# A graph attention and mixture-of-experts layer: an earlier first product, sums of exponentials made in all rows of a head's output, and a rearranged end of routing

## The chip, the cores and the metric

The kernel runs on one core of one Trainium2 chip. A core has five engines with queues of their own: TensorE (PE) multiplies matrices, VectorE (DVE) and ScalarE (ACT) compute on tiles, GpSimd (POOL) here mostly gathers and scatters rows by index, SyncE (SP) issues transfers. Tiles in SBUF have 128 partitions (rows); products land in PSUM. The metric is the device time of one execution in microseconds. A profiled execution of the kernel before took 2289.92 us, an unprofiled one 2153.45 us: all views of the trace belong to the longer, profiled one, and nothing in them tells where the difference lies.

## The reference

The first half is attention over a graph, with 8 heads of 64, on 4096 nodes of 512 features; the second is a feed-forward layer with 8 experts, of which each node uses two.

```python
def _L0_gnn_ref(node_matrix, adjacency_matrix, Wks, Wqs, Wvs, Wo):
    adj = jnp.maximum(adjacency_matrix, eye)
    q = jnp.einsum('nd,hdk->hnk', node_matrix, Wqs)      # k and v likewise
    scores = jnp.einsum('hqk,hmk->hqm', q, k) * kd ** (-0.5)
    scores = scores + IDENTITY_BIAS * eye - MASK_VAL * (1.0 - adj)
    att = jax.nn.softmax(scores, axis=-1)
    return jnp.einsum('hqm,hmk,hko->qo', att, v, Wo)

def _L0_ffn_ref(x, Wg, bg, W1, b1, W2, b2):
    logits = xf @ Wg + bg
    topk_scores, topk_idx = jax.lax.top_k(logits, 2)
    topk_w = jax.nn.softmax(topk_scores, axis=-1)
    h = jax.nn.gelu(jnp.einsum('nd,edh->neh', xf, W1) + b1, approximate=False)
    y = jnp.einsum('neh,ehf->nef', h, W2) + b2
    # the two chosen experts' rows of y, weighted by topk_w and added

x = x + _L0_gnn_ref(_layernorm(x), adj, ...)
x = x + _L0_ffn_ref(_layernorm(x)[None], ...)[0]
```

The graph is sparse. The kernel finds, for each tile of 128 query nodes, which nodes are neighbours of any of them, and gathers only those.

## The kernel before

The kernel has four stages. Stage one normalizes x, turns it, projects keys and values (to `kv_d` in memory) and queries (to `qT_d`), and beside this loads the adjacency matrix (32 pieces of 2 MB) and makes lists of neighbours from it, and packed masks. Stage two is the attention: 363 items, one for each query tile with itself (c < 0) and 331 with 128 listed key nodes each; an item is "full" if its keys concern all 128 queries of the tile, or "half" if only 64 of them. The end of a query tile (sums, reciprocal, output product, routing) is spread in pieces over the six items after its last; those of routing are jobs. The turn ends routing: rows are scattered to their expert's place in `xs_d`, blank rows are put after each expert's last, and a table tells each tile of 128 rows its expert and first row. The experts work off 69 such tiles.

`pk` and `kT` are an item's turned keys in PSUM and SBUF; `ps_e` is a pool of two PSUM tiles that the ends of tiles and the jobs share. Cuts are marked with `# ...`.

```python
# stage one: loads and the first block
xts = {}
def load_x1(i):
    xts[i] = work.tile([P, D], F32, tag="xt", bufs=6, name=f"xt_{i}")
    nc.sync.dma_start(out=xts[i], in_=x[ts(i, P), :])
for i in range(TPB):
    load_x1(i)
for n, src, queue in (("k", Wks, nc.scalar), ("v", Wvs, nc.scalar), ("q", Wqs, nc.sync)):
    for c in range(DC):
        queue.dma_start(out=w[n][:, c], in_=src[ts(c, P), :])
nc.sync.dma_start(
    out=wo, in_=Wo.rearrange("h k o -> (h k) o").rearrange("(c p) o -> p c o", p=P)
)
nc.sync.dma_start(out=wg[:, :, :E], in_=Wg.rearrange("(c p) e -> p c e", p=P))
nc.sync.dma_start(out=bg_sb, in_=bg.partition_broadcast(P))
# ...
def project_kv(b, t):
    i = b * TPB + t
    row = work.tile([P, 2, H * KD], F32, tag="kv", name=f"kv_{i}")
    for s, n in enumerate("kv"):
        pv = ps.tile([P, H * KD], F32, tag="mm", name=f"p{n}_{i}")
        for c in range(DC):
            nc.tensor.matmul(
                pv, xTs[b][:, c, ts(t, P)], w[n][:, c, :],
                start=(c == 0), stop=(c == DC - 1),
            )
        nc.scalar.copy(row[:, s], pv)
    nc.sync.dma_start(out=kv_d[ts(i, P), :], in_=row.rearrange("p s d -> p (s d)"))
# ...
for t in range(TPB):
    tokens_1(t)
    if t == 0:
        tokens_2(t)
        tokens_3(t)
for t in range(1, TPB):
    tokens_2(t)
    tokens_3(t)
for t in range(TPB):
    load_x1(TPB + t)
list_constants()
nc.sync.dma_start(out=out[N : N + P, :], in_=blank[:, :D])
# ...
def pack():
    i, c = ready.pop(0)
    m = work.tile([P, P], F32, tag="mask", bufs=5, name=f"pm_{i}_{c}")
    gather_mask(m, i, c)
    packed[i, c] = len(packed)
    nc.sync.dma_start(out=packed_at(i, c), in_=mask_part(m, i, c))
# ...
# keys of the masks, in lists_of
u = slice(at[i] + u0, at[i] + u1)
k = key[:, u0 - t0 : u1 - t0]
if h is None:
    nc.gpsimd.tensor_scalar_add(mask_of[:, u], k, float(i * (N + 1)))
else:
    nc.gpsimd.tensor_scalar(
        mask_of[:, u], k, 2.0, float(2 * i * (N + 1) + h),
        op0=ALU.mult, op1=ALU.add,
    )
# ...
# stage two: an item's keys are turned, its scores, exponentials and masks, its values
half_q = single.tile([P, 2, Q4], F32, name="half_q")
nc.vector.memset(half_q, 0.0)
spread = single.tile([P, NP, P], F32, name="spread")
nc.vector.memset(spread, 0.0)
for j in range(2):
    nc.vector.memset(half_q[:, j, j * Q4 // 2 : (j + 1) * Q4 // 2], 1.0)
for p in range(NP):
    u, j = divmod(p, 2)
    for r in range(2):
        row = (2 * u + r) * Q4 + j * Q4 // 2
        nc.vector.tensor_copy(
            spread[:, p, r * KD : (r + 1) * KD],
            ident[:, row : row + 1].to_broadcast([P, KD]),
        )
# ...
def turn(n):
    kT[n] = work.tile([P, NP, P], F32, tag="kT", bufs=3, name=f"kT_{n}")
    pk = ps_k.tile([P, 2, TB], F32, tag="k", name=f"pk_{n}")
    for p in range(NP):
        for r in range(2):
            half = slice(r * KD, (r + 1) * KD)
            nc.tensor.transpose(
                pk[:, r, ts(p, KD)], kv[n][half, ts(p, P)], ident[half, half]
            )
    nc.scalar.copy(
        kT[n].rearrange("k p (r j) -> k r p j", r=2),
        pk[:, :, : NP * KD].rearrange("k r (p j) -> k r p j", p=NP),
    )
# ... scores(n): products with q_in, then in ScalarE the exponentials of s into e
def masked(n):
    i, c = items[n]
    e, m = es[n], mask.pop(n)
    # ...
    nc.vector.tensor_mul(e, e, m.unsqueeze(1).to_broadcast(e.shape))
# ...
def values(n):
    i, c = items[n]
    e = es.pop(n)
    if c < 0:
        po[i] = ps_o.tile([P, NP, P], F32, tag="o", name=f"po_{i}")
    v = kv.pop(n)[:, H * KD :]
    q = queries(i, c)
    for h in range(H):
        p, r = divmod(h, 2)
        nc.tensor.matmul(
            po[i][r * KD : (r + 1) * KD, p, q], v[:, ts(h, KD)], e[:, h, :],
            start=(c < 0 and p == 0), stop=(c == listed[i] - 1),
            skip_group_check=True,
        )
    if c >= 0:
        nc.vector.tensor_add(acc[i][:, :, q], acc[i][:, :, q], e)
# ...
# pieces of a query tile's end, k items after its last
def piece(i, k):
    g = group_of[i]
    i0, m = groups[g]
    j = i - i0
    if k == 1:
        sums[i] = ps_e.tile([P, P], F32, tag="e", name=f"sums_{i}")
        a = acc.pop(i)
        for t in range(2):
            for q in range(4):
                u, r = divmod(q, 2)
                nc.tensor.matmul(
                    sums[i][q * Q4 : (q + 1) * Q4], half_q[:, t],
                    a[:, 2 * (2 * u + t) + r, :], start=(t == 0), stop=(t == 1),
                    tile_position=(0, q * Q4), skip_group_check=True,
                )
    if k == 2:
        rinv[i] = single.tile([P, P], F32, tag="rinv", name=f"rinv_{i}")
        nc.vector.reciprocal(rinv[i], sums[i])
        test = single.tile([P, P], F32, tag="test", name=f"test_{i}")
        nc.scalar.activation(test, sums.pop(i), AF.Copy, accum_out=fine[:, i, 0:1])
    if k == 3:
        rb[i] = ps_e.tile([P, NP, P], F32, tag="e", name=f"rb_{i}")
        for p in range(NP):
            nc.tensor.matmul(rb[i][:, p], spread[:, p], rinv[i], start=True, stop=True)
        test = single.tile([P, P], F32, tag="test", name=f"test2_{i}")
        nc.scalar.activation(test, rinv.pop(i), AF.Copy, accum_out=fine[:, i, 1:2])
    if k == 4:
        nc.vector.tensor_mul(osb[i], osb[i], rb.pop(i))
# ...
def later(n):
    busy = False
    for n0, i in left:
        piece(i, n - n0)
        busy = busy or n - n0 in (1, 3, 5)
    if jobs and not busy:
        then = jobs.pop(0)()
        if then:
            first_of_step.append(then)
# ...
if n + 3 < len(items):
    turn(n + 3)
if n + 2 < len(items):
    scores(n + 2)
values(n)
if c == listed[i] - 1:
    osb[i] = single.tile([P, NP, P], F32, tag="o", name=f"o_{i}")
    nc.scalar.copy(osb[i], po.pop(i))
later(n)
if n + 2 < len(items):
    masked(n + 2)
if c == listed[i] - 1:
    left.append((n, i))
# ...
# the end of routing
def finish_routing(pool, psum, blank):
    pn = psum.tile([P, E], F32, name="pn")
    nc.tensor.matmul(pn, ones, count, start=True, stop=True)
    many = pool.tile([P, E], F32, name="many")
    nc.vector.tensor_copy(many, pn)
# ...
past = pool.tile([P, NB, E], F32, name="past_e")
nc.vector.tensor_tensor(
    past, nth.unsqueeze(2).to_broadcast([P, NB, E]),
    upto.unsqueeze(1).to_broadcast([P, NB, E]), op=ALU.is_ge,
)
expert = pool.tile([P, NB], F32, name="expert")
nc.vector.tensor_reduce(expert, past, axis=AX.X, op=ALU.add)
nc.vector.tensor_mul(past, past, tiles_e.unsqueeze(1).to_broadcast([P, NB, E]))
nc.vector.tensor_reduce(first, past, axis=AX.X, op=ALU.add)
nc.vector.tensor_sub(first, nth, first)
nc.vector.tensor_scalar_mul(first, first, float(P))
nc.vector.scalar_tensor_tensor(
    first, expert, float(R), first, op0=ALU.mult, op1=ALU.add
)
nc.vector.tensor_scalar_min(first, first, float(E * R))
nc.vector.tensor_scalar_min(expert, expert, float(E - 1))
nc.vector.tensor_add(many, many, start_e)
nc.vector.tensor_copy(table[:, :NB], expert[:1])
nc.vector.tensor_copy(table[:, NB : 2 * NB], first[:1])
nc.vector.tensor_copy(table[:, 2 * NB :], many[:1])
nc.vector.tensor_add(first, first, number.to_broadcast([P, NB]))
nc.sync.dma_start(out=xs_d[E * R : E * R + P, :], in_=blank)
for e in range(E):
    last = nc.values_load(
        table[:, 2 * NB + e : 2 * NB + e + 1], engines=(SP,), min_val=e * R,
        max_val=e * R + N, skip_runtime_bounds_check_because=why,
    )
    s = nc.sync.dma_start(out=xs_d[bass.ds(last, P), :], in_=blank)
    for t in scatters:
        tc.declare_no_dep(s.ins, t.ins, reason="other rows")
    scatters.append(s)
```

The whole kernel:

Of the kernel before, what the change touches and what calls it, by code (L numbers as in the profile page):

```python
# [10 lines left out]
F32 = mybir.dt.float32  # L11
BF16 = mybir.dt.bfloat16
# [8 lines left out]
P = 128  # L21
# [22 lines left out]
def kernel(  # L44
# [106 lines left out]
    nc.gpsimd.iota(start_e, pattern=[[R, E]], base=0, channel_multiplier=0,  # L151
# [3 lines left out]
    for e in range(1, E):  # L155
# [9 lines left out]
    nth = const.tile([P, NB], F32, name="nth")  # L165
    nc.gpsimd.iota(nth, pattern=[[1, NB]], base=0, channel_multiplier=0,
                   allow_small_or_imprecise_dtypes=True)
# [4 lines left out]
    table = const.tile([1, 2 * NB + E], I32, name="table")  # L172
# [100 lines left out]
    with tc.tile_pool(name="wqkv", bufs=1) as wp, tc.tile_pool(name="p1", bufs=3) as work, tc.tile_pool(  # L273
# [12 lines left out]
        def load_x1(i):  # L286
            xts[i] = work.tile([P, D], F32, tag="xt", bufs=6, name=f"xt_{i}")
            nc.sync.dma_start(out=xts[i], in_=x[ts(i, P), :])

        for i in range(TPB):  # L290
            load_x1(i)
        for n, src, queue in (("k", Wks, nc.scalar), ("v", Wvs, nc.scalar), ("q", Wqs, nc.sync)):
            for c in range(DC):
                queue.dma_start(out=w[n][:, c], in_=src[ts(c, P), :])
        nc.sync.dma_start(
            out=wo, in_=Wo.rearrange("h k o -> (h k) o").rearrange("(c p) o -> p c o", p=P)
        )
        nc.sync.dma_start(out=wg[:, :, :E], in_=Wg.rearrange("(c p) e -> p c e", p=P))
        nc.sync.dma_start(out=bg_sb, in_=bg.partition_broadcast(P))
# [38 lines left out]
        def list_constants():  # L338
# [8 lines left out]
            for k in range(KV // D):  # L347
                nc.sync.dma_start(out=kv_d[N : N + 1, ts(k, D)], in_=blank[:1, :D])

        adj_in, flags, base, row_x, started, rows_of = {}, {}, {}, {}, {}, {}  # L350

        def load_adj(i):
            adj_in[i] = ap.tile([P, C, P], F32, tag="a", name=f"adjT_{i}")
            nc.sync.dma_start(out=adj_in[i], in_=adjT[i, :N].rearrange("(p c) q -> p c q", c=C))
# [147 lines left out]
        def list_keys(i, k):  # L502
# [21 lines left out]
            for h, u0, u1 in ((0, 0, a), (None, a, b), (1, b, listed[i])):  # L524
                u0, u1 = max(u0, t0), min(u1, t0 + m)
                if u0 < u1:
                    u = slice(at[i] + u0, at[i] + u1)
                    k = key[:, u0 - t0 : u1 - t0]
                    if h is None:
                        nc.gpsimd.tensor_scalar_add(mask_of[:, u], k, float(i * (N + 1)))  # L530
                    else:
                        nc.gpsimd.tensor_scalar(
# [55 lines left out]
        def project_kv(b, t):  # L588
# [26 lines left out]
        for t in range(1, TPB):  # L615
            tokens_2(t)
            tokens_3(t)
# [850 lines left out]
```

## Time and profile before

| What | Value |
|---|---|
| time, median of 3 | 2153.45 us (2150.13 to 2153.85) |
| span of the profiled execution | 2288.2 us |
| granted TensorE clock, mean | 0.961 of full |
| stage one, by the trace | 0 to about 460 us |
| attention | 460 to 1703 us |
| turn | 1703 to 1740 us |
| experts | 1740 to 2281 us |
| memory traffic | 398.85 MB read, 76.90 MB written |

The profile lists instructions by engine and by line of the kernel, each with its duration and with what ended the idle time ahead of it on its engine: `[9.63 <-POOL mask_of L532]` says that the engine stood idle for 9.63 us until GpSimd's instruction of line 532, which writes `mask_of`, was done. Matrix products are pipelined: what one costs is the distance of starts, not its own duration. A product of two float32 operands shows as two records, so eight products are 16. Idle time of an engine that does not set the end costs nothing.

### The profile page before, as it was taken

What the parts mean: (1) busy time and instruction counts of PE and PEld (TensorE: products, weight loads), DVE (VectorE), ACT (ScalarE), POOL (GpSimd) and SP (SyncE); (2) the same over time, 40 slices, a digit from 0 to 9 for tenths busy, and PEclk for the clock granted to TensorE, in tenths of its full rate; (3) what the DMA queues carried; (4) which work ended last, traced back from release to release, by engine and by line L of the source; (5) the groups of instructions that cost most, each with busy time, mean ns of one, the idle gap of its engine ahead of it and who ended that gap; (6) DMA issues with size and microseconds to landing.
All of it is one profiled execution on the core that took longest, in us unless ns stands there. A gap on an engine that the chain in (4) does not pass through costs nothing. (4 is left out here: it accounts for less than half of the span.)

```text
span 2288.2 us, 48475 instructions
## 1 busy us (share of the span) xinstructions
PE 2090.1 (91%) x18748; PEld 1385.6 (61%) x18748; DVE 1262.7 (55%) x2289; ACT 932.1 (41%) x1703; POOL 1026.6 (45%) x1078
## 2 busy tenths in 40 slices
PE   7988997889999989999999999899965999999998
PEld 3434443377777777777777777776742444444443
DVE  4786666266666657665756767566672323333232
ACT  2544443354455545544445445444531222222221
POOL 1044434766666565556565655557630212112121
PEclk9998999999999999999999999999987999999999
DMA  7877787667777777777887877766766655555554
GB/s 293 318 268 265 255 287 247 179 204 214 224 229 237 225 232 228 221 227 226 236 231 233 244 210 219 227 201 199 216 235 167 133 138 139 138 131 138 137 133 90
DMA packets 213232, 479.04 MB, mean 209 GB/s; under 512 B 49106, under 2 KB 81106, under 8 KB 208900
## 3 DMA queue, kind: packets, MB, share of 16 engines
q0 software_dynamic: 78944, 241.65, 37.2%
q1 hardware_dynamic: 132900, 232.10, 32.5%
q8 instruction: 153, 2.51, 0.4%
q10 hardware_dynamic: 1152, 2.10, 0.3%
q14 instruction: 83, 0.68, 0.1%
HBM read 398.85 MB, written 76.90 MB: 208 GB/s over the span
## 5 line engine op out<-in xcount | busy, mean ns | idle before, releaser
L230 POOL DMA_INDIRECT kv<-kv_d,key_of x363 | 405.5, 1117 | 389.5 <-PE po L993 233.2
L981 DVE TENSOR_TENSOR e<-e,mask 128x512 f32<-128x512 f32 (+1 forms) x363 | 322.5, 889 | 301.0 <-ACT e L973 145.5
L926 ACT COPY kT<-pk 128x512 f32<-128x512 f32 x395 | 232.2, 588 | 378.5 <-PE pk L923 221.2
L993 PE MATMUL po<-e,kv 128*64 128x64 f32 (+1 forms) x5808 | 327.0, 251 | 21.7 <-issue 20.8
L999 DVE TENSOR_TENSOR acc<-acc,e 128x512 f32<-128x512 f32 (+1 forms) x363 | 321.0, 884 | 2.2 <-PE po L993 1.0
L230 POOL DMA_INDIRECT mask<-in_adjT_dram,mask_of x234 | 282.2, 1206 | 72.8 <-issue 63.4
L1395 POOL DMA_INDIRECT out_dram<-y,r x69 | 107.5, 1558 | 457.0 <-ACT y L1394 426.1
L993 PEld LDWEIGHTS po<-e,kv 128*64 128x64 f32 x5808 | 254.4, 140 | 74.0 <-issue 30.9
L970 PE MATMUL s<-q,kT 128*128 128x128 f32 x1832 | 278.7, 297 | 0.9 <-issue 0.7
L1359 PE MATMUL ph<-w,xT 128*128 x552 | 251.3, 598 | 1.0 <-ACT xT L209 1.0
L1388 PE MATMUL py<-w,hT 128*128 x552 | 248.4, 593 | 0.9 <-DVE hT L1373 0.9
L970 PEld LDWEIGHTS s<-q,kT 128*128 128x128 f32 x1832 | 233.1, 199 | 18.9 <-issue 2.8
L923 PE MATMUL pk<-ident,kv 64*128 64x64 f32 x2904 | 177.2, 240 | 48.7 <-issue 27.2
L923 PEld LDWEIGHTS pk<-ident,kv 64*128 64x128 f32 x2904 | 123.9, 142 | 120.9 <-issue 81.4
L230 POOL DMA_INDIRECT pm<-in_adjT_dram,mask_of x129 | 126.0, 977 | 155.0 <-DMA packed_h<-pm 78.5
L963 ACT ACTIVATE e<-s 128x512 f32<-128x512 f32 x268 | 147.3, 597 | 72.2 <-PE s L958 28.6
L361 DVE TENSOR_REDUCE flags<-adjT 128x64 f32<-128x4096 f32 x32 | 141.1, 4411 | 60.3 <-DMA adjT<-in_adjT_dram 60.2
L973 ACT ACTIVATE e<-s 128x512 f32<-128x512 f32 x229 | 137.6, 601 | 82.5 <-PE s L970 51.6
L1393 DVE TENSOR_TENSOR y<-py,bb 128x512 f32<-128x512 f32 x69 | 47.7, 692 | 219.2 <-PE py L1388 219.2
L958 PE MATMUL s<-q,kT 64*128 64x128 f32 x2144 | 163.8, 286 | 3.9 <-issue 2.3
L1359 PEld LDWEIGHTS ph<-w,xT 128*128 128x128 f32 x552 | 100.3, 192 | 101.7 <-issue 100.1
L1388 PEld LDWEIGHTS py<-w,hT 128*128 128x128 f32 x552 | 99.6, 190 | 101.1 <-issue 100.0
(599 smaller groups left out, 2595.4 us busy)
## 6 DMA issues: line engine op xcount, KB each, us to landing
adjT<-in_adjT_dram SPq DMA_DIRECT2D x32, 2048.0 KB
bb<-in_L_ffn_b_dram SPq DMA_DIRECT2D x138, 256.0 KB
r<-xs_d SPq DMA_DIRECT2D x69, 258.0 KB
kv_d<-kv SPq DMA_DIRECT2D x32, 512.0 KB
xt<-in_x_dram SPq DMA_DIRECT2D x32, 256.0 KB
qT_d<-qT SPq DMA_DIRECT2D x8, 1024.0 KB
q<-qT_d SPq DMA_DIRECT2D x64, 128.0 KB
xr<-in_x_dram SPq DMA_DIRECT2D x32, 256.0 KB
```

The lines of the kernel that those rows point to most:

```text
L230: nc.gpsimd.indirect_dma_start(out=to, out_offset=None, in_=src, in_offset=bass.IndirectOffsetOnAxis(ap=of[:, at[i] + c : at[i] + c + 1], ...
L361: nc.vector.tensor_reduce(flags[g][:, :, j, :], adj_in.pop(i).rearrange("p c (h q) -> p h c q", h=2), axis=AX.X, op=ALU.max,)
L923: nc.tensor.transpose(pk[:, r, ts(p, KD)], kv[n][half, ts(p, P)], ident[half, half])
L926: nc.scalar.copy(kT[n].rearrange("k p (r j) -> k r p j", r=2), pk[:, :, : NP * KD].rearrange("k r (p j) -> k r p j", p=NP),)
L958: nc.tensor.matmul(s[r][:, p, :], k[rows, p, :], q_in[i][rows, p, r, :], start=True, stop=True,)
L963: nc.scalar.activation(e.rearrange("p (a r) q -> p r a q", r=2)[:, r], s[r], AF.Exp)
L970: nc.tensor.matmul(s[:, p], k[:, p, :], q_in[i][:, p, :, q], start=True, stop=True)
L981: nc.vector.tensor_mul(e, e, m.unsqueeze(1).to_broadcast(e.shape))
L993: nc.tensor.matmul(po[i][r * KD : (r + 1) * KD, p, q], v[:, ts(h, KD)], e[:, h, :], start=(c < 0 and p == 0), stop=(c == listed[i] - 1), s ...
L999: nc.vector.tensor_add(acc[i][:, :, q], acc[i][:, :, q], e)
L1359: nc.tensor.matmul(ph, xTs[b][:, c, :], w1[:, bass.ds(es[b], 1), c, :], start=(c == 0), stop=(c == DC - 1),)
L1388: nc.tensor.matmul(py, hTs[b][:, c, :], w2[:, bass.ds(es[b], 1), c, :], start=(c == 0), stop=(c == HC - 1),)
```

## The change

It has four parts. First, the start: one transfer for each weight matrix, and issued in another order; the turns of tiles 1 to 3 come between the products of the first block, and weights and blank rows that are needed later are moved in unit nine of stage one. Stores are issued a unit later than they were, and masks have seven buffers. Second, keys of the masks of the last group of tiles are computed on VectorE. Third, sums of exponentials: `acc` was multiplied by columns of ones of 32, so that a sum came to stand in 16 rows, and after the reciprocal four products spread the inverses over the 64 rows of each head. Now a product with 64 columns of ones gives each sum in all 64 rows of its head, and the reciprocal, now of 128x512 in two halves, can be multiplied with the output directly. Fourth, the end of routing: an expert's last tile of rows is moved back so that it ends with the last row (`begin`), rows that it shares with the tile before are sent to spare rows of the output (`mine`, `spare`), and so no blank rows are needed after the counts are known; the table is computed in memory that no other tile used before.

```diff
-    xts[i] = work.tile([P, D], F32, tag="xt", bufs=6, name=f"xt_{i}")
+    xts[i] = work.tile([P, D], F32, tag="xt", bufs=5, name=f"xt_{i}")
     nc.sync.dma_start(out=xts[i], in_=x[ts(i, P), :])
+adj_in, flags, base, row_x, started, rows_of = {}, {}, {}, {}, {}, {}
+def load_adj(i):
+    adj_in[i] = ap.tile([P, C, P], F32, tag="a", name=f"adjT_{i}")
+    nc.sync.dma_start(out=adj_in[i], in_=adjT[i, :N].rearrange("(p c) q -> p c q", c=C))
+def load_w(n, src, queue):
+    queue.dma_start(out=w[n], in_=src.rearrange("(c p) d -> p c d", p=P))
+load_w("k", Wks, nc.scalar)
 for i in range(TPB):
     load_x1(i)
-# ... the loads of the weights, wo, wg and bg as above
+load_w("v", Wvs, nc.sync)
+load_adj(0)
+load_w("q", Wqs, nc.sync)
+load_x1(TPB)
+def load_more():
+    nc.sync.dma_start(
+        out=wo, in_=Wo.rearrange("h k o -> (h k) o").rearrange("(c p) o -> p c o", p=P)
+    )
+    nc.sync.dma_start(out=wg[:, :, :E], in_=Wg.rearrange("(c p) e -> p c e", p=P))
+    nc.sync.dma_start(out=bg_sb, in_=bg.partition_broadcast(P))
+    for k in range(KV // D):
+        nc.sync.dma_start(out=kv_d[N : N + 1, ts(k, D)], in_=blank[:1, :D])
+    nc.sync.dma_start(out=out[N : N + P, :], in_=blank[:, :D])
+    for e in range(E + 1):
+        nc.sync.dma_start(out=xs_d[e * R : e * R + P, :], in_=blank)
...
+engine = nc.vector if i >= NT - G else nc.gpsimd
 if h is None:
-    nc.gpsimd.tensor_scalar_add(mask_of[:, u], k, float(i * (N + 1)))
+    engine.tensor_scalar_add(mask_of[:, u], k, float(i * (N + 1)))
 else:
-    nc.gpsimd.tensor_scalar(
+    engine.tensor_scalar(
         mask_of[:, u], k, 2.0, float(2 * i * (N + 1) + h),
         op0=ALU.mult, op1=ALU.add,
...
+stores = []
+def project_kv(b, t, between):
...
         nc.scalar.copy(row[:, s], pv)
-    nc.sync.dma_start(out=kv_d[ts(i, P), :], in_=row.rearrange("p s d -> p (s d)"))
+        if s == 0 and between:
+            between()
+    stores.append(lambda: nc.sync.dma_start(
+        out=kv_d[ts(i, P), :], in_=row.rearrange("p s d -> p (s d)")))
...
-for t in range(1, TPB):
-    tokens_2(t)
-    tokens_3(t)
-for t in range(TPB):
-    load_x1(TPB + t)
+load_x1(TPB + 1)
 list_constants()
-nc.sync.dma_start(out=out[N : N + P, :], in_=blank[:, :D])
...
-m = work.tile([P, P], F32, tag="mask", bufs=5, name=f"pm_{i}_{c}")
+m = work.tile([P, P], F32, tag="mask", bufs=7, name=f"pm_{i}_{c}")
 gather_mask(m, i, c)
 packed[i, c] = len(packed)
-nc.sync.dma_start(out=packed_at(i, c), in_=mask_part(m, i, c))
+stores.append(lambda: nc.sync.dma_start(
+    out=packed_at(i, c), in_=mask_part(m, i, c)))
...
+while stores:
+    stores.pop(0)()
+if u in load_at and u:
     load_adj(load_at[u])
+if u == 9:
+    load_more()
...
+    between = None
+    if b == 0 and s < 3:
+        tokens_2(s + 1)
+        if s < 2:
+            load_x1(TPB + 2 + s)
+        between = lambda: tokens_3(s + 1)
+    project_kv(b, s, between)
 else:
     if s == 4:
         qT = block.tile([P, NP, TB], F32, tag="qT", name=f"qT_{b}")
     project_q(b, s - 4, qT)
     if s == 7:
-        nc.sync.dma_start(out=qT_d[:, :, ts(b, TB)], in_=qT)
+        stores.append(lambda b=b, qT=qT: nc.sync.dma_start(
+            out=qT_d[:, :, ts(b, TB)], in_=qT))
...
+end = pool.tile([P, E + 1], F32, name="end")
+nc.vector.memset(end[:, E:], float(E * R + P))
+nc.vector.tensor_add(end[:, :E], many, start_e)
+more_e = pool.tile([P, E], F32, name="more_e")
+nc.vector.tensor_sub(more_e, end[:, 1:], end[:, :E])
+ends = pool.tile([P, NB, E], F32, name="ends")
+nc.vector.tensor_mul(ends, past, more_e.unsqueeze(1).to_broadcast([P, NB, E]))
+till = pool.tile([P, NB], F32, name="till")
+nc.vector.tensor_reduce(till, ends, axis=AX.X, op=ALU.add)
...
+nc.vector.tensor_scalar(till, till, end[:, 0:1], -float(P), op0=ALU.add, op1=ALU.add)
+begin = pool.tile([P, NB], F32, name="begin")
+nc.vector.tensor_tensor(begin, first, till, op=ALU.min)
 nc.vector.tensor_copy(table[:, :NB], expert[:1])
-nc.vector.tensor_copy(table[:, NB : 2 * NB], first[:1])
-nc.vector.tensor_copy(table[:, 2 * NB :], many[:1])
-nc.vector.tensor_add(first, first, number.to_broadcast([P, NB]))
-# ... all of the blank rows, to scatters.append(s)
...
-half_q = single.tile([P, 2, Q4], F32, name="half_q")
-# ... to the end of the loop that fills spread
...
-    sums[i] = ps_e.tile([P, P], F32, tag="e", name=f"sums_{i}")
+    sums[i] = ps_e.tile([P, NP, P], F32, tag="e", name=f"sums_{i}")
     a = acc.pop(i)
-    # ... the eight products with half_q, and all of k == 2 and k == 3
+    for h in range(H):
+        p, r = divmod(h, 2)
+        nc.tensor.matmul(
+            sums[i][r * KD : (r + 1) * KD, p], ones32, a[:, h, :],
+            start=True, stop=True, skip_group_check=True,
+        )
+if k in (2, 3):
+    if k == 2:
+        rinv[i] = single.tile([P, NP, P], F32, tag="rinv", name=f"rinv_{i}")
+    half = slice((k - 2) * NP // 2, (k - 1) * NP // 2)
+    nc.vector.reciprocal(rinv[i][:, half], sums[i][:, half])
+    if k == 3:
+        test = single.tile([P, NP, P], BF16, tag="test", name=f"test_{i}")
+        nc.scalar.activation(
+            test, sums.pop(i), AF.Copy, accum_out=fine[:, i, 0:1]
+        )
 if k == 4:
-    nc.vector.tensor_mul(osb[i], osb[i], rb.pop(i))
+    test = single.tile([P, NP, P], BF16, tag="test", name=f"test2_{i}")
+    nc.scalar.activation(test, rinv[i], AF.Copy, accum_out=fine[:, i, 1:2])
+    nc.vector.tensor_mul(osb[i], osb[i], rinv.pop(i))
...
-busy = busy or n - n0 in (1, 3, 5)
+busy = busy or n - n0 in (1, 5)
...
+end_cm = tc.tile_pool(name="end", bufs=1, side="right")
+endp = end_cm.__enter__()
+nth = endp.tile([P, NB], F32, name="nth")
...
-with tc.tile_pool(name="end", bufs=1) as pool, tc.tile_pool(
-    name="ps_end", bufs=1, space=PSUM
-) as psum:
-    finish_routing(pool, psum, blank)
+first_scatters = list(scatters)
...
+with tc.tile_pool(name="ps_end", bufs=1, space=PSUM) as psum:
+    finish_routing(endp, psum)
...
+to = work.tile([P, 2], F32, tag="to", bufs=8, name=f"to_{b}")
+nc.vector.scalar_tensor_tensor(
+    to[:, 0:1], r[:, D : D + 1].bitcast(I32), spare, mine[:, b : b + 1],
+    op0=ALU.subtract, op1=ALU.mult,
+)
+nc.vector.tensor_add(to[:, 1:2].bitcast(I32), to[:, 0:1], spare)
 nc.gpsimd.indirect_dma_start(
     out=out,
-    out_offset=bass.IndirectOffsetOnAxis(
-        ap=r[:, D : D + 1].bitcast(I32), axis=0
-    ),
+    out_offset=bass.IndirectOffsetOnAxis(ap=to[:, 1:2].bitcast(I32), axis=0),
     in_=y, in_offset=None, compute_op=ALU.add,
```

## The prediction

> **What bounds the kernel now.** I read the page's first two parts, then busy time by stage, then the time-ordered view where one stage passes to the next, then one query tile's end. The page:
>
> ```profile
> PE 2090.1 (91%) x18748; PEld 1385.6 (61%) x18748; DVE 1262.7 (55%) x2289; ACT 932.1 (41%) x1703; POOL 1026.6 (45%) x1078
> ```
>
> The busy windows, in the columns of their heading:
>
> ```profile
> core 0: us, PE busy (x) PEld busy (x) DVE busy (x) ACT busy (x) POOL busy (x), PEclk, DMA share, GB/s
> 0.00:20.00 20.00, 4.22 (x16) 3.04 (x17) 11.14 (x63) 5.99 (x8) 8.79 (x115) 1.00 0.92 326
> ...
> 460.00:1703.00 1243.00, 1161.10 (x15462) 933.46 (x15462) 811.36 (x1322) 614.77 (x1219) 738.28 (x639) 0.97 0.74 221
> ...
> 1740.00:2281.00 541.00, 537.51 (x1652) 264.15 (x1652) 163.44 (x343) 128.09 (x208) 105.98 (x68) 0.99 0.58 133
> ```
>
> TensorE is busy 93% of the attention (1161.10 of 1243) and 99% of the experts (537.51 of 541). It idles in the first 20 us and in the turn (1703 to 1740). So a gain is either TensorE work taken out of the attention, or a hole closed. The beginning and the two seams, in order of time:
>
> ```profile
> 9.37 1.28 ACT L202 ACT_TABLE_LOAD   x1 [9.37 <-DMA wq<-in_L_gnn_Wqs_dram]
> 20.00 1.06 PE L594 MATMUL pk<-wk,xT 128*128 128x512 f32 x1
> 459.59 0.59 ACT L926 COPY kT<-pk 128x512 f32<-128x512 f32 x1 [9.63 <-POOL mask_of L532]
> 460.22 0.09 DVE L883 MEMSET ones<- 128x32 f32 x1 [16.06 <-DMA qT_d<-qT]
> 1720.69 0.17 DVE L815 COPY many<-pn 128x8 f32<-128x8 f32 x1 [5.41 <-PEq L1211]
> 1723.60 6.47 SPq L861 DMA_DIRECT2D xs_d<-blank  x8
> 1735.50 0.38 SPq L1345 DMA_DIRECT2D r<-xs_d  x1
> ```
>
> One query tile's end, in order of time (sums, reciprocal, spread, product with o):
>
> ```profile
> 549.31 0.64 PE L1018 MATMUL sums<-acc,half_q 128*32 128x128 f32 x16
> 549.89 0.46 PE L923 MATMUL pk<-ident,kv 64*128 64x64 f32 x8
> 550.47 0.95 DVE L1025 RECIPROCAL rinv<-sums 128x128 f32<-128x128 f32 x1
> 554.53 1.16 PE L1031 MATMUL rb<-rinv,spread 128*128 128x128 f32 x8
> 555.62 0.46 PE L923 MATMUL pk<-ident,kv 64*128 64x64 f32 x8
> 556.09 0.69 DVE L1035 TENSOR_TENSOR o<-o,rb 128x512 f32<-128x512 f32 x1
> ```
>
> From one start to the next, sums cost TensorE 0.58 us (549.31 to 549.89), the spread 1.09 (554.53 to 555.62).
>
> **The Trainium skill.** "TensorEngine Tiling (Array Packing)", Key Properties: a free size of 32 lets four column tiles run side by side, 64 two. The trace agrees: 16 records at 128*32 take 0.58 us, the value product's 16 at 128*64 take 1.02 (548.29 to 549.31). "VectorE: DVE Perf Modes", First, the fixed hardware budget: a reciprocal is an iterative divide with a repeat count of eight. The trace agrees that it is dear: 0.951 us for 128x128, against 0.69 for a product over 128x512. "PSUM — Partial Sum Buffer", Engine vs sequencer instructions: ScalarE's and VectorE's queues are strictly first in, first out; so an instruction put in wrongly early holds all behind it. In the trace the 9.63 us wait at 459.59 is of this kind. "DMA: Bandwidth & Descriptors", Issuing engines are not separate DMA queues: another issuing engine saves only issue time. Here ScalarE's first work starts at 9.37, when its own queue has issued the weights.
>
> **Part 1, the beginning.** ScalarE's queue spends 4.88 and 4.40 us on issuing wk and wv in pieces, so its table load waits until 9.37, xn of tile 0 until 10.67; then four tiles are turned before the first product at 20.00. After: one issue on ScalarE, and only tile 0 is turned ahead. x of tile 0 lands at 4.67 and its mean and variance are done at 7.89; xn to about 8.8, four transposes (1.08) to 10.0, copy (0.59) to 10.6, product at about 10.7: 9.3 earlier. The transposes of tiles 1 to 3 come back between products, about 0.5 each: 9.3 − 1.5 = −7.8. The mask tiles go from 5 buffers to 7 and stores are issued a unit later, in the same order on the queue; the waits that this can shorten (the queue's for packed masks 156.1 us, GpSimd's 78.5) are mostly not TensorE's, so −2. At unit nine, 3.6 MB of weights and blank rows (1 MB wo, 256 KB of out, nine of 258 KB) are now moved in the middle of the stage: 10 us of DMA at the 390 GB/s seen in the turn, where adjacency loads wait in the same queue: +1.
>
> **Part 2, the seam to the attention.** The last group's keys of masks are made on VectorE, not on GpSimd behind 13 gathers (about 1.25 us apart). That wait (ends at 459.59) goes, but the first acc exponential also needs the last store of qT_d, landed by 460.22 (the 16.06). What is left is VectorE's constants (half_q, spread, to 462.0), which go or shrink: the first exponential, at 464.15 before, at about 460.3 after: −4.
>
> **Part 3, the sums.** Removed per tile: 0.58 + 1.09 us of TensorE; added: eight products 64 wide, 1.02. 32 × (1.67 − 1.02) = −20.8 if all of it counts. Added on VectorE: reciprocals of 128x256 twice instead of 128x128 once. Slope from 128x2 at 0.17 us and 128x128 at 0.951: (0.951 − 0.17)/126 = 6.2 ns a column, so 0.17 + 254 × 6.2 ns = about 1.75 each; +2.55 a tile, 82 us of VectorE in all; its share goes from 65% to 72%, which it can bear on average. ScalarE's two tests grow from 0.27 and 0.31 to about 0.59: +0.6 a tile.
>
> But locally it may not bear it. The test of the sums is issued in the third step after a tile's end, reads the same PSUM tile as the second reciprocal and waits for it; next in ScalarE's queue is the next kT copy, and the transposes' one PSUM buffer waits for that. Steps: two half mask products or additions and one more at a pitch of 0.61 plus 2 × 1.75 = 5.3 us on VectorE from the start of the second step; test 0.8, kT copy 0.59: 6.7. TensorE wants the buffer after three half steps of 2.09, at 6.3: a stall of 0.4 in 18 tiles. Where the third listed key tile is full (14 tiles), its mask product is 0.54 longer: 7.3 against about 6.3, a stall of 1.0 to 1.1. 18 × 0.4 + 14 × 1.1 = +23. Routing jobs may now run in the third step; nine of those take a PSUM tile that the second reciprocal must free first: 9 × 0.9 = +8. Some of these 31 lies in holes that are there already (TensorE's 7% idle, 82 us); I take them as 29. Attention: −21 + 29 = +8, and the tail of the last tile: reciprocal to product was 1689.29 to 1692.26, 2.97, and becomes 2 × 1.75 + 0.1 + 0.68 = 4.3: +1.3.
>
> **Part 4, the turn.** VectorE's chain starts at 1720.69, though counts were ready at 1712.85: it waited for the last store of out (memory to be reused). After, it has memory of its own. Gone too: the blank rows' nine stores on SyncE's queue (1722.12 to 1730.1), now at unit nine. The chain from 1720.69 to 1726.64 grows by a product (0.75), a reduction (0.75) and six small ones, to 7.9 us. What does not move: w2's 8 MB fill DMA (395 GB/s) until about 1720.5, and the last scatters must land. Estimate: counts read at 1716 to 1721, tables at 1724 to 1729, the first rows asked for at 1729 to 1731, not 1735.5: −5.
>
> **Part 5, the experts.** Two VectorE operations of about 0.2 us a tile, beside TensorE at 99%: 0.
>
> Sum: −7.8 − 2 + 1 − 4 + 8 + 1.3 − 5 = −8.5. Profiled execution took 2289.92, unprofiled 2153.45; nothing shows where profiling adds the 136 us, so a gain read in the attention may be smaller without it. Waits are the parts that shrink most likely; I round to −10, or 2143.
>
> **Rivals.** A: the reciprocals hide wholly; then −20.8, and −16.5 from the other parts, give 2116. For it: VectorE idles 35% in the attention, and mostly waits for exponentials (145.5 us), not the other way. Against: at tile ends no slack is left by the count above. B: VectorE and ScalarE become the bound at tile ends and stall TensorE by some 1.6 us a tile: 51 − 21 = +30, with −16.5 2167. For it: one PSUM buffer for transposes; against: TensorE waits only 17.8 us for kT now. C: the beginning's gain is eaten, since the adjacency loads pace stage one (VectorE waits 60.2 us for them) and the weights are moved into their midst: 2151.
>
> **Range and chances.** A range of 2113 to 2168 holds A, B and C. Faster by over 2% is below 2110.4, beyond A: 0.07. Slower by over 2% is above 2196.5, which no rival reaches: 0.04. The rest 0.89.
>
> **What would show it.** First product near 10.7 and the attention beginning some 9 to 13 us earlier (parts 1 and 2); a stretch of DMA near full at unit nine; sums 16 records in 1.02, reciprocals near 1.75 twice, no rb; waits of TensorE's transposes for kT or of ScalarE's test for the reciprocal, 20 to 30 us in all (if near zero, A); first expert rows asked for some 10 us after VectorE reads the counts, against 14.8 (1720.69 to 1735.50); experts still 7.8 us a tile. Wrong would be a step of the attention that gets longer away from tile ends, or a stage one as long as before.

## The result, and the profile after

| | us, median | range |
|---|---|---|
| before | 2151.79 | 2146.38 to 2153.85 |
| after | 2101.81 | 2099.46 to 2103.25 |

The ratio is 0.977, with a 95% interval of 0.9748 to 0.9793: 50 us less, where 10 were predicted, and below the range of 2113 to 2168.

One thing has to be known ahead of all comparisons. Chips differ: on the chips of the experiments the kernel before took 2150.28 us on one and 2285.72, 2286.42, 2293.98 and 2302.88 us on four others. By its time the profile ahead of the prediction, of 2289.92 us, is one of the longer kind, while the 2153.45 us beside it, and the profile after, are of the shorter. The two profiles can't be compared stage by stage. In what follows each run is compared with the kernel before on its own chip, and stages only between chips of the same kind.

The page of the kernel after, busy time of each engine:

```profile
PE 1995.2 (95%) x18492; PEld 1328.0 (63%) x18492; DVE 1360.8 (65%) x2466; ACT 954.0 (45%) x1703; POOL 1040.4 (50%) x1067
```

VectorE has 98 us more than the 1262.7 of before: 112.2 of reciprocals in place of about 30, and the two small operations of each expert tile. The first 20 us in the busy windows, columns as in the prediction's:

```profile
0.00:20.00 20.00, 10.98 (x25) 5.32 (x26) 9.76 (x59) 4.57 (x6) 8.77 (x115) 1.00 0.91 344
```

TensorE works 10.98 us of the first 20, not 4.22. And in order of time the first product, one tile's end, and the turn:

```profile
10.11 1.22 PE L610 MATMUL pk<-wk,xT 128*128 128x512 f32 x1 [0.68 <-ACT xT L210]
...
491.66 1.04 PE L1033 MATMUL sums<-acc,ones 128*64 128x128 f32 x16
492.63 0.46 PE L938 MATMUL pk<-ident,kv 64*128 64x64 f32 x8
492.75 1.76 DVE L1042 RECIPROCAL rinv<-sums 128x256 f32<-128x256 f32 x1
496.06 1.75 DVE L1042 RECIPROCAL rinv<-sums 128x256 f32<-128x256 f32 x1
497.84 0.60 ACT L1045 ACTIVATE test<-sums 128x512 bf16<-128x512 f32 x1 [0.93 <-DVE rinv L1042]
...
1537.43 0.17 PE L839 MATMUL pn<-count,ones 128*128 128x8 bf16 x1 [7.75 <-PEq L1229]
1537.63 0.17 DVE L841 COPY many<-pn 128x8 f32<-128x8 f32 x1 [6.43 <-PE pn L839]
1545.91 0.37 SPq L1362 DMA_DIRECT2D r<-xs_d  x1
```

The first product starts at 10.11. Reciprocals take 1.75 us, and ScalarE's test does wait for the second. From the counts to the first rows it is 8.28 us (1537.63 to 1545.91), not 14.81. All this is near the forecast; none of it makes 50 us.

### The profile page after: what moved, and what is told of

The parts are those of the page before. It is cut to its first block, busy times and chain, and to the rows that moved or that the text cites. A ratio compares the mean times of both kernels' runs of the same rounds, so it can differ in the third digit from the quotient of the medians.

```text
span 2101.5 us, 48040 instructions
## 1 busy us (share of the span) xinstructions
PE 1995.2 (95%) x18492; PEld 1328.0 (63%) x18492; DVE 1360.8 (65%) x2466; ACT 954.0 (45%) x1703; POOL 1040.4 (50%) x1067
## 5 line engine op out<-in xcount | busy, mean ns | idle before, releaser
L231 POOL DMA_INDIRECT kv<-kv_d,key_of x363 | 428.7, 1181 | 228.0 <-PE po L1008 128.2
L1419 POOL DMA_INDIRECT out_dram<-y,to x69 | 107.7, 1561 | 454.8 <-ACT y L1411 450.9
L231 POOL DMA_INDIRECT mask<-in_adjT_dram,mask_of x234 | 274.6, 1173 | 71.3 <-issue 50.9
L1008 PE MATMUL po<-e,kv 128*64 128x64 f32 (+1 forms) x5808 | 305.7, 248 | 0.0
L985 PE MATMUL s<-q,kT 128*128 128x128 f32 x1832 | 268.1, 290 | 2.7 <-ACT acc L978 2.7
L1008 PEld LDWEIGHTS po<-e,kv 128*64 128x64 f32 x5808 | 241.4, 138 | 44.0 <-issue 0.2
L985 PEld LDWEIGHTS s<-q,kT 128*128 128x128 f32 x1832 | 224.3, 193 | 18.4 <-ACT acc L978 2.8
L938 PE MATMUL pk<-ident,kv 64*128 64x64 f32 x2904 | 168.3, 236 | 22.4 <-ACT kT L941 22.1
L938 PEld LDWEIGHTS pk<-ident,kv 64*128 64x128 f32 x2904 | 118.5, 139 | 86.9 <-issue 46.1
L1411 ACT ACTIVATE y<-y,gate 128x512 f32<-128x512 f32 x69 | 49.8, 722 | 230.5 <-DVE y L1410 226.1
L973 PE MATMUL s<-q,kT 64*128 64x128 f32 x2144 | 152.6, 280 | 0.0
```

The source lines that it names most:

```text
L231: nc.gpsimd.indirect_dma_start(out=to, out_offset=None, in_=src, in_offset=bass.IndirectOffsetOnAxis(ap=of[:, at[i] + c : at[i] + c + 1], ...
L938: nc.tensor.transpose(pk[:, r, ts(p, KD)], kv[n][half, ts(p, P)], ident[half, half])
L973: nc.tensor.matmul(s[r][:, p, :], k[rows, p, :], q_in[i][rows, p, r, :], start=True, stop=True,)
L985: nc.tensor.matmul(s[:, p], k[:, p, :], q_in[i][:, p, :, q], start=True, stop=True)
L1008: nc.tensor.matmul(po[i][r * KD : (r + 1) * KD, p, q], v[:, ts(h, KD)], e[:, h, :], start=(c < 0 and p == 0), stop=(c == listed[i] - 1), s ...
```

## The experiments

My theory at first: stage one gains by its earlier start alone, the sums cost about as much as they save, the turn gives some 5 us. The rivals: the reciprocals hide and TensorE's 21 us count; or something in the middle of stage one gains.

**The kernel before, three times again**, for profiles beside those of the experiments: no edit.

> The kernel before, unchanged, for a second profile. Theory one (the first profile caught an unusually long execution): a span of about 2150 us, the attention near 1120 us and not 1243, stage one near 430 and not 450, TensorE's clock near 0.98. Theory two (profiling itself lengthens this kernel): a span again near 2290 us.

> The kernel before again, for its profile beside these. Theory one (each chip has its own time, and the profiles of one chip can be compared with each other only): where it takes about 2286 us, ScalarE again stands idle without a visible cause for over 1 us some 14 times in the attention; where it takes about 2152 us, hardly ever, and the attention is over 100 us shorter. Theory two (a matter of the execution, not of the chip): both kinds turn up on one chip.

> The kernel before, for a profile beside the others of this chip. If the buffers' gain is one block's: from the first product of the seventh block to that of the eighth 60 us or more, where with seven buffers it was 46 us on another chip, and the first six blocks alike within 3 us.

They took 2288.02, 2292.53 and 2303.95 us on three chips, 1.0012, 1.0000 and 1.0006 of the kernel before beside them. The profiled execution among the first took 2281.94 us, no more than those beside it, so profiling does not lengthen the kernel. Theory one of the first expectation has the cause wrong as well: on each of the five chips all executions of the kernel before, 7 to 57 of them, were of one kind, so it goes with the chip and not with the execution. The third came from a chip of the longer kind, where the seventh block of stage one is 68.9 us long (first products at 340.1 and 409.0 us). The first six blocks are not alike within 3 us of those with seven buffers, as I had expected: they start up to 10 us later (340.1 against 330.1 for the seventh), but the two runs are of different kinds of chips.

**Each part alone, on the kernel before.** Stage one (loads, order, late stores, seven mask buffers, weights in unit nine):

```diff
-tag="mask", bufs=5
+tag="mask", bufs=7
-nc.sync.dma_start(out=packed_at(i, c), in_=mask_part(m, i, c))
+stores.append(lambda: nc.sync.dma_start(out=packed_at(i, c), in_=mask_part(m, i, c)))
 # and all else of stage one in the change, but blank rows of xs_d and mask_of
```

> The kernel before with the changes of stage one alone: loads, turns between products, stores a unit later, seven mask buffers, weights moved in unit nine (no blank rows of xs_d there). Theory one (part 1 as predicted): -8 to -10 us, all from the first product, which comes 10 us earlier. Theory two (the seven buffers and late stores also take waits out of the middle of the stage): -20 us or more, with the distance from the first product of the first block to that of the last below that of the kernel before by over 8 us.

2252.27 us against 2285.72: 0.9853 (0.9827 to 0.9879), −33 us. Theory two holds. (A block is four tiles of 128 rows; stage one has eight.) The distance from the first block's product to the last one's fell from 382.6 us to 362.5. Nearly all of these 20 us lie in one block. The busy windows of the seventh block, first in the kernel before on this chip, then with stage one changed:

```profile
337.00:402.30 65.30, 50.17 (x207) 23.50 (x203) 43.37 (x83) 20.59 (x34) 29.37 (x44) 0.93 0.74 241
```

```profile
326.00:372.30 46.30, 46.30 (x207) 22.35 (x204) 36.86 (x76) 20.71 (x35) 25.51 (x40) 1.00 0.80 266
```

The same 207 records of products take 65.3 us, TensorE idle for 15 of them and its mean granted clock 0.93, and then 46.3 us without a hole.

The sums alone:

```diff
-rinv[i] = single.tile([P, P], F32, tag="rinv", name=f"rinv_{i}")
+rinv[i] = single.tile([P, NP, P], F32, tag="rinv", name=f"rinv_{i}")
 # and all else of the sums in the change, jobs in the third step too
```

> The kernel before with the sums alone: products 64 wide, two reciprocals of 128x256, no spread, jobs in the third step. Theory one (my prediction: the test behind the second reciprocal stalls TensorE): +5 to +10 us. Theory two (the reciprocals hide, TensorE's time counts): -15 to -25 us. Theory three (what was removed also waited or broke TensorE's clock): below -25 us.

2296.80 against 2285.72: 1.0064 (1.0041 to 1.0087), +11 us, on this chip a little above the +5 to +10 of my theory.

The end of routing alone:

```diff
-nc.sync.dma_start(out=xs_d[E * R : E * R + P, :], in_=blank)   # and eight more, after the counts
+for e in range(E + 1):                                         # at unit nine
+    nc.sync.dma_start(out=xs_d[e * R : e * R + P, :], in_=blank)
 # and all else of the end of routing in the change
```

> The kernel before with the end of routing alone: no blank rows after the counts, own memory for the table, blank rows of xs_d written at unit nine of stage one, duplicates sent to spare rows. Theory one (as predicted): -5 to -7 us. Theory two (it also costs in stage one or the experts): -3 us or more.

2278.60 against 2285.72: 0.9976 (0.9955 to 0.9996), −7 us, as expected (the interval is −1 to −10).

**The changed kernel, and parts taken out of it.** In the second, the old sums; in the third, the old stage one:

```diff
-ones32, products of 64, rinv of 128x512, busy in (1, 5)
+half_q, spread, rinv of 128x128, busy in (1, 3, 5)
```

```diff
-tag="mask", bufs=7
+tag="mask", bufs=5
 # and loads, order and stores of stage one as before
```

> The changed kernel again. In the first experiments the kernel before took 2286 us, 6% more than the 2152 us of the first comparison. If the parts add (stage one -33, sums +11, end of routing -7) and nothing else matters: 2250 to 2260 us where the kernel before takes 2286 us. If the large gain of the first comparison holds everywhere: 0.977 of whatever the kernel before takes.

> The changed kernel with the old sums: 32-wide products, reciprocal of 128x128, spread product, no jobs in the third step. If the sums cost time as they did alone (+11 us): 8 to 14 us shorter than the changed kernel. If they pay where TensorE has no other holes (rival A): 15 to 25 us longer.

> The changed kernel with stage one as before (old loads and order, five mask buffers, stores at once; blank rows of xs_d at unit nine; masks' last keys still on VectorE). If stage one is the whole gain, as it was alone: 30 to 36 us longer than the changed kernel. If only the earlier first product counts: 8 to 10 us longer.

Against 2293.98 us, the changed kernel took 2254.22: 0.983 (0.9785 to 0.9875); with old sums 2240.91: 0.9781 (0.9731 to 0.9832); with the old stage one 2284.97: 0.9956 (0.994 to 0.9972). So stage one is the larger part of the gain here too (0.9956 − 0.983 is 29 us). The three parts alone, −33, +11 and −7, sum to −29; the whole gives −40 (−29 to −49), so its interval just reaches their sum. For the sums the two intervals overlap. Repeated on another chip, the version with old sums gave 0.9839 (0.9796 to 0.9883):

> The changed kernel with the old sums, again. On a chip that takes 2150 us for the kernel before: from the first tile's sums to the last one's the new sums took 1014.0 us, the old ones in the run with seven buffers alone 1017.9; so 2 to 8 us above the changed kernel, 0.978 to 0.981. On one that takes 2286: 0.978 again.

On chips of the longer kind the new sums are thus no measurable gain, and within the changed kernel no sure loss either; only alone they were slower beyond the interval.

**What in stage one does it.** The start alone (stores at once, five mask buffers), and the late stores alone (loads as before, five buffers):

```diff
-stores.append(store)      # issued at the start of the next unit
+store()                   # the start alone
```

```diff
-nc.sync.dma_start(out=packed_at(i, c), in_=mask_part(m, i, c))
+stores.append(lambda: nc.sync.dma_start(out=packed_at(i, c), in_=mask_part(m, i, c)))
 # likewise kv_d and qT_d; nothing else
```

> The kernel before with the start alone (one load a weight, turns between products, weights in unit nine), stores at once and five mask buffers. If late stores make the rest of the gain: -8 to -12 us, with the sixth block as long as before (about 65 us from its first product to that of the next). If the start makes it all: -28 us or more.

> The kernel before with the late stores alone (kv_d, qT_d and packed masks are issued at the start of the next unit; loads as before, five mask buffers). If the rest of stage one's gain (33 us less the 10 of the earlier first product) is that the queue no longer stands at a store whose gather has not landed: -12 to -23 us, with SyncE's waits for pm below half of before. If it needs the seven buffers or comes from the loads: within 5 us of before.

Against 2286.42 us: 2279.63 for the start, 0.9972 (0.9956 to 0.9988), −7 us, with the seventh block still 68.3 us; 2286.81 for the late stores, 1.0003 (0.9986 to 1.002), nothing. So late stores do not free the queue by themselves. The start alone had five buffers of x as well, so one buffer of x fewer is not the gain either. What remained was the number of mask buffers:

```diff
-xts[i] = work.tile([P, D], F32, tag="xt", bufs=6, name=f"xt_{i}")
+xts[i] = work.tile([P, D], F32, tag="xt", bufs=5, name=f"xt_{i}")
-m = work.tile([P, P], F32, tag="mask", bufs=5, name=f"pm_{i}_{c}")
+m = work.tile([P, P], F32, tag="mask", bufs=7, name=f"pm_{i}_{c}")
```

> The kernel before with seven mask buffers instead of five (and five of x instead of six), stores at once. If the buffers alone let the queue go on: -20 to -28 us. If they only help together with the late stores: within 6 us of before.

> The kernel before with seven mask buffers and late stores together, start as before. If these two make the larger part of stage one's gain: -20 to -28 us, the seventh block (from its first product to that of the eighth) below 55 us and SyncE's waits for pm under 35 us there. If the start is needed as well: above -12 us.

Against 2150.28 us (the chip of the shorter kind): 2119.06 with seven buffers alone, 0.9859 (0.9837 to 0.9881), −31 us; 2120.33 with late stores as well, 0.9858 (0.9835 to 0.9881). Two numbers in the kernel give 31 of the 50 us, a little more than forecast. Late stores add nothing here either: with them SyncE waits 115.2 us for pm in stage one, without them 116.8. The seventh block takes 46.1 us in both, as forecast, but SyncE's waits for pm did not fall below 35 us (46.6 between 320 and 418 us).

The chain is seen in the waits of stage one, 20 to 450 us. Of the kernel before on the chip of 2285.72 us, on GpSimd, SyncE's queue, VectorE and ScalarE in turn (total us, times, longest; `packed_h` and `packed_d` are the packed masks in memory, `pm` a mask in its buffer, L632 its store):

```profile
POOL pm L230 <- DMA packed_h<-pm: 77.6, 19, 9.4
...
SPq L632 <- DMA pm<-in_adjT_dram,mask_of: 164.3, 56, 7.7
...
DVE flags L361 <- DMA adjT<-in_adjT_dram: 62.7, 15, 10.7
...
ACT started L477 <- DVE past_b L436: 51.3, 7, 18.1
```

With seven buffers alone, on the chip of 2150.28 us:

```profile
POOL pm L230 <- DMA packed_h<-pm: 31.1, 12, 8.1
...
SPq L632 <- DMA pm<-in_adjT_dram,mask_of: 116.8, 62, 7.0
...
DVE flags L361 <- DMA adjT<-in_adjT_dram: 29.4, 8, 10.1
...
ACT started L477 <- DVE past_b L436: 36.0, 8, 8.4
```

With all of stage one changed, on the first one's own chip, the same four are 27.2, 75.3, 8.4 and 36.3 us.

With five, GpSimd's gather waits until the store of an earlier mask has landed and its buffer is free; the store of the new one, in SyncE's queue, waits for that gather; the loads of adjacency stand behind it in the same queue. The loads themselves wait little: for what VectorE must finish first, 4.9 us in all. So the queue falls back, and the last adjacency load goes out at 384.5 us; with seven buffers at 358.0, the kernel otherwise the same:

```profile
L354 SPq DMA_DIRECT2D adjT<-in_adjT_dram x32: 332/384/737, 18.5 to 384.5; - x32
```

```profile
L354 SPq DMA_DIRECT2D adjT<-in_adjT_dram x32: 328/382/1015, 18.0 to 358.0; - x32
```

(The first line is of a chip of the longer kind, the second of the other; on the first one's own chip, with all of stage one changed, it was 353.6. No kernel with five buffers was profiled on the other kind, so where in stage one its 31 us lay is not shown.) And how a late load comes about and gets to TensorE, in order of time, in the kernel before:

```profile
342.01 4.18 SPq L632 DMA_DIRECT2D packed_h<-pm  x2
...
343.09 0.94 POOL L230 DMA_INDIRECT pm<-in_adjT_dram,mask_of  x1 [6.88 <-DMA packed_h<-pm]
...
346.29 0.37 SPq L354 DMA_DIRECT2D adjT<-in_adjT_dram  x1
...
354.70 4.42 DVE L361 TENSOR_REDUCE flags<-adjT 128x64 f32<-128x4096 f32 x1 [2.54 <-DMA adjT<-in_adjT_dram]
...
362.62 0.16 DVE L436 TENSOR_SCALAR past_b<-base 128x12 f32<-128x12 f32 x1
...
362.87 2.27 ACT L477 ACTIVATE started<-slots,past_b 128x640 bf16<-128x640 int16 x3 [18.14 <-DVE past_b L436]
...
365.50 0.58 ACT L598 COPY kv<-pv 128x512 f32<-128x512 f32 x1
365.65 3.24 PE L594 MATMUL pv<-wv,xT 128*128 128x512 f32 x4 [3.95 <-ACT kv L598]
```

The gather stood 6.88 us for a buffer; the second of the two stores goes out after it, and only then the load, at 346.29. The reduction of that load starts late since it came late; past_b stands behind it in VectorE's queue; ScalarE stands for 18.14 us at an operation that needs past_b, and the copies that empty TensorE's PSUM tiles stand behind it; TensorE waits 3.95 us for such a copy. That is the smaller part of the 15 us for which TensorE idles in this block. The larger one, 9.8 us, are products of the lists that wait for VectorE's own operations behind such a reduction:

```profile
PE pb L392 <- DVE x L386: 7.1, 2, 4.9
...
PE pr L496 <- DVE key L517: 2.7, 1, 2.7
```

More buffers still, on the version with old sums:

```diff
-tag="mask", bufs=7
+tag="mask", bufs=9
```

> The same with nine mask buffers. If SyncE's queue still stands at packed stores (49 us of waits for pm were left in the last 100 us of the stage with seven) and TensorE feels it: 5 to 12 us below seven buffers. If the stage is paced by TensorE and ScalarE by now: within 3 us.

2256.99 against 2302.88: 0.9804 (0.976 to 0.9849), beside 0.9839 with seven on the same chip. The medians are 6 us apart, and the four executions of each do not overlap. But the first block's product to the last one's took 364.2 us with nine and 361.1 with seven, so stage one shows nothing of it; where the 6 us come from is not shown.

**What the new sums lose.** Three runs: the test of the sums a step later; no job in the third step; and the old sums with idle reciprocals.

```diff
-if k == 3:
-    nc.scalar.activation(test, sums.pop(i), AF.Copy, accum_out=fine[:, i, 0:1])
 if k == 4:
+    nc.scalar.activation(test, sums.pop(i), AF.Copy, accum_out=fine[:, i, 0:1])
```

```diff
-busy = busy or n - n0 in (1, 5)
+busy = busy or n - n0 in (1, 3, 5)
```

```diff
 # old sums, k == 2:
 nc.vector.reciprocal(rinv[i], sums[i])
+nc.vector.reciprocal(idle[:, :P], idle[:, :P])
 # k == 3:
+nc.vector.reciprocal(idle, idle)
```

> The changed kernel with the test of the sums a step later, beside that of the inverses, so that it no longer stands behind the second reciprocal in ScalarE's queue. If that stall is what makes the sums dear (they cost 11 to 13 us, TensorE's work is 21 us less, so 32 to 34 us are lost): 15 us or more below the changed kernel, 0.975 of before or less. If VectorE's 82 us of reciprocals are the loss: within 6 us of the changed kernel's 0.983.

> The changed kernel with no job in the third step of a tile's end, as before. By my count nine jobs wait there for the second reciprocal, 0.9 us each: 5 to 8 us below the changed kernel, so about 0.980 of before. If jobs gain by more places: at or above 0.983.

> The changed kernel with the old sums and two idle reciprocals a tile that nobody reads, of 128x128 in the second step and of 128x256 in the third, so that VectorE works as long as with the new sums. With old sums it was 0.978 of before, with new 0.983. If VectorE's time is what the new sums lose: 0.991 to 0.995 (30 us more than without, as TensorE's 21 us are not saved). If it hides: 0.976 to 0.981, and the loss lies in ScalarE's tests and PSUM tiles held longer.

The late test: 2252.09 against 2286.42, 0.9849 (0.9791 to 0.9907). No gain over 0.983, on a chip of the longer kind, though ScalarE's waits of the test for the reciprocal fell from 13.3 us (11 times) to 3.8 (once). No jobs in the third step: 2259.12, 0.9891 (0.9845 to 0.9938): no better, so the jobs lose nothing measurable by that place. The idle reciprocals, on the chip of the shorter kind: 2105.75 against 2150.28, 0.9792 (0.9773 to 0.9812), within the 0.976 to 0.981 that stood for hiding. On chips of that kind, from the first tile's sums to the last one's, the kernel with seven buffers and old sums took 1017.9 us, with late stores as well 1015.4 (the attention's code is the same), the one with old sums and idle reciprocals 1022.9, the changed kernel 1014.0. So 84 us of VectorE's time (0.894 and 1.743 us, 32 times each) cost 5 to 7.5 us.

The stall that I forecast is there, in the waits of the attention with old sums (seven buffers alone) and in the changed kernel, both of chips of the shorter kind:

```profile
PE pk L923 <- ACT kT L926: 9.4, 5, 3.1
```

```profile
PE pk L938 <- ACT kT L941: 20.6, 23, 2.6
...
ACT test L1045 <- DVE rinv L1042: 35.1, 31, 3.9
```

ScalarE stands behind the reciprocal in 31 tiles of 32, 35.1 us; TensorE's waits for kT grow by 11.2 us, a third of that. With the idle reciprocals, behind which no test stands, TensorE's waits for kT are 9.9 us, so what reaches TensorE in these waits is not VectorE's time but ScalarE's standing behind it. The late test was not run on a chip of this kind, so whether these 11 us can be had stays open.

## Why the prediction was wrong

Part by part, between the kernel before with seven buffers alone (span 2118.0) and the kernel after (span 2101.5), both of the shorter kind; the times are starts in their traces:

| Stretch | seven buffers | after | difference |
|---|---|---|---|
| to the last product of stage one | 419.3 | 412.6 | −6.7 |
| to the first acc exponential | 10.9 | 8.6 | −2.3 |
| to the first tile's sums | 69.6 | 70.5 | +0.9 |
| to the last tile's sums | 1017.9 | 1014.0 | −3.9 |
| to the first expert product | 51.4 | 45.2 | −6.2 |
| to the end | 548.9 | 550.6 | +1.7 |

Together −16.5, and the seven buffers −31: 48 of the 50 us. The sum of the prediction was −8.5, so about 40 us were missed: 29 at the buffers (−2 forecast) and nearly all of the rest at the sums (+8 forecast, −3.0 in the table).

**The step that failed** is a sentence of part 1: the waits that seven buffers and late stores can shorten "are mostly not TensorE's, so −2". It was −31, and all of it from the buffers. I had the two waits in hand, 156.1 us of SyncE's queue and 78.5 of GpSimd's, and asked who waits directly. I did not follow the queue on: the adjacency loads stand in it behind the stores, I had VectorE's 60.2 us of waits for those loads on the list too, and used them for rival C, as if the loads paced the stage by themselves. The late-running loads were the fault of the masks. In the profile ahead of the prediction the seventh block is 68.0 us long and the sixth 51.3; a look at these distances would have shown where stage one stood.

The other steps:

- Part 1, the start: product at 10.7 forecast, 10.11 found. −7.8 forecast, and +1 for the weights at unit nine; alone −7 (0.9972), and −6.7 in the table. Right.
- Part 2, the seam: −4 forecast, −2.3 in the table. On the shorter kind of chip the stretch is 10.9 us in both traces without the change and 8.6 and 9.0 in both with it; on the longer kind it is 13.8 to 16.1 in nine without and 13.6 to 15.4 in seven with it. So about −2 on the one, and no clear gain on the other.
- Part 3, the sums: reciprocals of 1.75 us as worked out from two sizes, TensorE's product 0.97 us (491.66 to 492.63) for the 1.02 assumed. The stall was forecast at 29 us net against 21 saved, +8. On the shorter kind of chip it was mis-sized: of the 21.7 us that 31 tiles save (0.58 + 1.09 − 0.97 each) 17.8 were lost beside the run with seven buffers, 20.3 beside the one with late stores as well, and not 29; TensorE's waits for kT are 11.2 of them. On the longer kind the sums alone cost 11 us, near the +8, but there the run that took the stall away gained nothing, so this nearness may be luck. So rival A, in which all of 21 us counts, did not come true anywhere, and neither did B.
- Part 4, the turn: −5 forecast, −6.2 in the table and −7 alone. But the counts are read no earlier (31.9 us after the last tile's sums, 32.7 before): VectorE waits for the count's product instead of the store of out, and that product now stands behind the branch on `again` in TensorE's queue (`PEq L1229`, 7.75 us idle), ahead of which it stood before. In the trace ahead of the prediction VectorE's wait is put down to that branch too (`PEq L1211`), with seven buffers to a store of out (5.60 us): the store was only one of two things that ended late. Whether it would gain to put it ahead of the branch again was not tried. What is gained is the chain behind it, 8.28 us to the first rows and not 13.81 (1550.44 to 1564.25 with seven buffers). Half the reason was right.
- Part 5: 0 forecast, +1.7 in one execution each; the run with late stores and seven buffers has the 550.6 of after too, so nothing is shown.
- The discount on stage two for profiling ("nothing shows where profiling adds the 136 us") rested on two kinds of chips taken for one. It changed the sum by 1.5 us, so it is not what failed, but the trace that I read stage two from was not that of the time I predicted.

Whether the changed kernel would be better off with the old sums stays open: with them it has 0.9781 and 0.9839 where it has 0.983 with the new ones, all on the longer kind. On the shorter kind that version was not run; there the old sums' stretch is 1 to 4 us longer.

## What to carry to other kernels

A wait of a queue is not worth what its direct waiters lose: ask what else stands behind it in the same queue, and who needs that. Where a tile is gathered by one queue, stored by another and given back only when the store has landed, count the buffers against the whole round trip; here two more of 64 KB each gave 31 us, three times the whole forecast. And before stages of two profiles are set beside each other, see that the kernel before takes the same time on both chips.

## What the runs showed of the hardware that was not expected

The two kinds of chips run the same program 6 to 7% apart, and nearly all of the difference is in the attention. The changed kernel, profiled on both, takes 1014.0 us from the first tile's sums to the last one's on the shorter kind and 1139.0 on the longer (granted clock 0.99 and 0.97 there); stage one takes 412.6 and 420.1, the experts 550.6 and 550.1. Waits of ScalarE and VectorE there, in the kernel before on a chip that took 2285.72 us (a releaser named "remote" or "issue" is one that the profile does not see):

```profile
ACT kT L926 <- remote: 38.9, 13, 6.0
```

```profile
DVE e L981 <- issue: 75.9, 56, 4.0
```

And with seven buffers, the attention's code the same, on the chip of 2150.28 us:

```profile
DVE e L981 <- issue: 8.9, 9, 1.2
```

There ScalarE has no wait of the first sort at all. One such hole, in order of time, on the longer kind:

```profile
829.54 0.35 PE L993 MATMUL po<-e,kv 128*64 128x64 f32 x4 [1.07 <-issue]
...
832.50 0.58 ACT L926 COPY kT<-pk 128x512 f32<-128x512 f32 x1 [5.97 <-remote]
833.14 0.69 PE L923 MATMUL pk<-ident,kv 64*128 64x64 f32 x8 [3.26 <-ACT kT L926]
```

The copy's keys had been in PSUM since before 827 us (their product started at 825.89), and ScalarE began it at 832.50; TensorE stopped within a row of products that wait for nothing. What holds the engines on these chips was not found, and no run was made to find it.
